# Turning the first stage's fourteen masks by DMA instead of on TensorE, in a four-layer graph network on one core

## Chip, core and metric

One core of one Trainium2 chip runs the whole program. The metric is the device time of one execution in microseconds (us); before the change the median of three runs is 2909.86 us (2909.22 to 2911.19).

## The reference, cut to what matters

The inputs are `x` (2708 x 512, float32) and an adjacency matrix `adj` (2708 x 2708, int32, symmetric, about 2.3% ones). Four layers follow each other, each `x = layernorm(x + gnn(x, adj))`. Only the first layer bears on the change:

```
Ab = adj > 0
keep = Ab & (cumsum(Ab, axis=1) <= 64)          # the first 64 neighbours of each row
nb_mean = (keep @ x) / max(keep.sum(axis=1), 1)
xj = leaky_relu(nb_mean @ W_nb.T + b_nb)
xi = leaky_relu(x @ W_line.T + b_line)
x = layernorm(x + xi + where(cnt > 0, xj, 0))
```

The second layer uses `Ab` without the limit of 64; the third and fourth are attention layers over the same mask.

## The kernel before

The 2708 rows are cut into 22 tiles of up to 128 rows (`NT = 22`, `P = 128`; the last tile, `LAST = 21`, has 20 rows). The kernel keeps the transposed mask of the whole graph in one fp8 tile, `maskT`, with the columns of one tile of rows side by side. The first layer has two stages.

**First stage** (the loop `for t in range(NT)` under `l0a`). For each tile `t` of rows:

- TensorE transposes the rows of `x` (four 128x128 blocks, line L133) and ScalarE copies them out as `xT` (L135). This is done one tile ahead.
- TensorE multiplies `xT` by `W_nb.T` (L259, "the first product" below). ScalarE writes the result rounded to fp32r as `yH` (L231) and VectorE the rest as `yL` (L236).
- TensorE multiplies `xT` by `W_line.T` (L259, "the second product"). VectorE adds the bias (L363) and applies leaky ReLU (L195); POOL's queue stores the result (L365). The second product has one PSUM buffer, so that of tile t+1 waits for the bias addition of tile t.

Beside this, 14 of the 22 masks (`HERE = NT - 8`) are made in this stage, at t = 2 to 6, 8 to 12 and 14 to 17 ("mask iterations"); t = 7, 13 and 18 to 21 make none, and t = 7 and t = 13 are called gaps here. For one mask of 128 rows:

- POOL's queue loads it from `adj` as bf16 (L272) into a buffer `m`, one of three.
- ScalarE takes a sigmoid over all 2708 columns, which also counts the ones (`count`, L277).
- VectorE runs a scan and a multiplication over the first half of the columns, and again over the second half (`place`, L283 and L286). The first scan waits for `count`; the scan of the second half continues the first. They are called scan 1, multiplication 1, scan 2 and multiplication 2.
- `turn_here` transposes the finished mask on TensorE in 22 blocks (L295) into PSUM, and ScalarE takes the sign of what stands there, in four pieces (8, 8, 5 and 1 blocks, L299), into `maskT`. POOL's queue then copies a few rows of the last block (L302).

**Second stage** (`l0b`). The masks' columns of four tiles at a time are expanded by ScalarE (`kept`, L380) and TensorE accumulates mask x (yH + yL) over all 22 tiles (L516). The remaining 8 masks are made beside it by `other_masks`, and these are turned by DMA already: `turn` (L307, on SP's queue) writes the transposed blocks into free memory, and `signs` (L312) is ScalarE's pass from there into `maskT`.

The order on each engine is fixed when the program is built: a scheduler lays the instructions out in each engine's queue, and each queue is worked off in order at run time. A few orders are forced by hand: `pe` ties TensorE's instructions of the first stage into the order in which they are written, and `tc.issue_after` holds `count` and `place` behind named instructions.

Of the kernel before, what the change touches and what calls it, by code (L numbers as in the profile page):

```python
# [2 lines left out]

# [27 lines left out]
def kernel(  # L31
# [18 lines left out]
    def rows(t):  # L50
        return min(P, N - t * P)
# [151 lines left out]
    with ExitStack() as phase:  # L203
# [5 lines left out]
        gate = yp.tile([P, 1], F32, name="gate")  # L209
        nc.vector.memset(gate, -STEP / 2)  # L210
        weight2 = yp.tile([P, KD, D], F32, name="weight2")
        yH = yp.tile([P, NT, D], F32R, name="yH")
        yL = yp.tile([P, NT, D], F32R, name="yL")
        nc.gpsimd.memset(yH[:, NT - 1, :].bitcast(F32), 0.0)
        nc.gpsimd.memset(yL[:, NT - 1, :].bitcast(F32), 0.0)

        ps_tr = phase.enter_context(tc.tile_pool(name="ps_tr", bufs=2, space=PSUM))
        ps_mm = phase.enter_context(tc.tile_pool(name="ps_mm", bufs=1, space=PSUM))
# [9 lines left out]
        highs = {}  # L228

        def keep_y(t, n, pm):  # L230
            highs[t] = nc.scalar.copy(yH[:n, t, :], pm[:n])  # L231
            if t == LAST:
                low = slice(TWIN, TWIN + n)
                nc.scalar.copy(yL[low, t, :], pm[low])
                return nc.vector.tensor_sub(yH[low, t, :], pm[low], yL[low, t, :].bitcast(F32))
            return nc.vector.tensor_sub(yL[:n, t, :], pm[:n], yH[:n, t, :].bitcast(F32))  # L236

        def halves(j):

# [30 lines left out]
        def load_mask(i, m):  # L270
            n = rows(turns[i])
            nc.gpsimd.dma_start(m[:n, :N], adj[turns[i] * P:turns[i] * P + n, :], max_dma_last_dim=N * 2)  # L272
            return m
# [11 lines left out]
                                         OP.add, OP.min)  # L285
            return nc.vector.tensor_mul(m[:n, c0:c1], m[:n, c0:c1], places[:n, :c1 - c0])  # L286

        def turn_here(i, m, psum, order=as_it_comes):
            t, n = turns[i], rows(turns[i])
            for g0 in range(0, NT, G):  # L290
                g1 = min(g0 + G, NT)
                ps = psum()
                for j in range(g0, g1):
                    w = rows(j)
                    order(nc.tensor.transpose(ps[:w, j - g0, :n], m[:n, j * P:j * P + w], identb[:n, :n]))  # L295
                parts = [(P, g0, min(g1, FULL))] + ([(rows(FULL), FULL, NT)] if g1 > FULL else [])
                for w, a, b in parts:
                    if a < b:
                        nc.scalar.activation(maskT[:w, a:b, t * P:t * P + n], ps[:w, a - g0:b - g0, :n], AF.Sign,  # L299
                                             saturate=False)  # L300
                if g1 == NT:
                    nc.gpsimd.dma_start(maskT[TWIN:TWIN + few, LAST, t * P:t * P + n],  # L302
                                        maskT[:few, LAST, t * P:t * P + n])
                yield

        def turn(i, m, into):
            nc.sync.dma_start_transpose(into, m)  # L307

# [11 lines left out]
        with ExitStack() as ph:  # L320
            st = ph.enter_context(tc.tile_pool(name="l0a", bufs=1))
            wnT, wlT = weight(), weight2
            room = [maskT[:, G + k, :4 * D].bitcast(F32) for k in range(2 * KD)]

            xs = rows_of(x)
            xTs = early(0, NT, lambda t, order=as_it_comes: transposed(ahead, ps_tr, xs(t), rows(t), "xT", order))

            transpose_weight(room[:KD], ps_tr, wnT, l0_w_nb, (nc.sync, nc.scalar))  # L330
            lows = {}
            for t in range(2):
                xT = xTs(t, order=pe)
# [3 lines left out]
            masks = early(1, HERE, lambda i: load_mask(i, st.tile([P, N], BF16, name="m", bufs=3)))  # L337
# [3 lines left out]
            counted = turned = 0  # L341
            for t in range(NT):
                n = rows(t)
                if t > 1:

                    lows[t] = keep_y(t, n, product(xTs(t, order=pe), n, wnT, 0, pe, sums() if t % 2 else None))
                xT = xTs(t)
                if t + 1 < NT:
                    xTs(t + 1, order=pe)
                while turned < counted - (t + 2 < NT):  # L350
                    for _ in turn_here(turned, masks(turned), lambda: sums(BF16, (P, G, P)), pe):
                        pass
                    turned += 1
# [9 lines left out]
                nc.vector.tensor_add(u[:n], pm[:n], b_line[:n])  # L363
                low = rows_made = leaky(u[:n], u[:n])
                nc.gpsimd.dma_start(r0_dram[t * P:t * P + n, :], u[:n])  # L365
                if now:
                    with tc.issue_after(low.ins):
                        place(counted, m, places, 1, 2)
                    counted += 1

        with ExitStack() as ph:
# [132 lines left out]
            for i, b in enumerate(cuts):  # L506
                ts_ = range(*b)
                pa = {t: sums() for t in ts_}
                for j in range(NT):
                    if j + 1 < NT:  # L510
                        nxt, nxt_made = kept(b, j + 1)
                    elif i + 1 < len(cuts):
                        nxt, nxt_made = kept(cuts[i + 1], 0)
                    for t in ts_:
                        for y in halves(j):
                            nc.tensor.matmul(pa[t], kT[:, (t - b[0]) * P:(t - b[0] + 1) * P], y[:, j, :],  # L516
                                             start=(j == 0 and y is yH), stop=(j == LAST))
# [12 lines left out]
                todo = finish(ts_, us)  # L530
# [23 lines left out]
        with ExitStack() as ph:  # L554
            st = ph.enter_context(tc.tile_pool(name="l1b", bufs=2))
            for t in range(NT):
                n = rows(t)
                x1 = fetched(x1_dram, t, n, st, "x1")
                z1 = fetched(z1_dram, t, n, st, "z1")
                pa = sums()  # L560
                for g0 in range(0, NT, G):
                    g1 = min(g0 + G, NT)
                    mf = st.tile([P, G, P], F32R, name="mf")
                    nc.scalar.copy(mf[:, :g1 - g0, :], maskT[:, g0:g1, t * P:(t + 1) * P])  # L564
                    for j in range(g0, g1):
                        for y in halves(j):
                            nc.tensor.matmul(pa, mf[:, j - g0, :], y[:, j, :],  # L567
                                             start=(j == 0 and y is yH), stop=(j == LAST))
# [959 lines left out]
```

## Time and profile before

| What | Value |
|---|---|
| Median of three runs | 2909.86 us (2909.22 to 2911.19) |
| The profiled execution's own time | 2911.22 us |
| Its span on the core | 2909.0 us |
| TensorE busy | 2827.0 us, 97% of the span |
| VectorE busy | 1983.5 us, 68% |
| ScalarE busy | 1501.7 us, 52% |
| POOL busy | 247.5 us, 9% |
| Mean granted TensorE clock | 0.996 |

The first stage takes the first 207 us of the span. The rest is not touched by the change. Shares over the whole span are averages over stages with different limits, so the first stage has to be read by itself: in stretches of time, and instruction by instruction on each engine's timeline.

### The profile page before, as it was taken

To read this page: it belongs to the slowest core of one execution; us is meant where nothing else is said; L and a number is where in the kernel's file an instruction comes from. 1 tells how busy PE (TensorE), PEld (TensorE's weight loads), DVE (VectorE), ACT (ScalarE), POOL (GpSimd) and SP (SyncE) were. 2 spreads that over 40 slices of the span, in tenths; PEclk is the share of its full clock that TensorE was granted. 3 is DMA by queue.
4 is the path that set the end of the run, shared out by engine and by line. 5 is a ranking of instruction groups with operands and counts; after the bars stand their busy time and mean duration, and the time that the engine had idled before them with its cause. 6 is when DMAs were issued, how large, how long until landed. Compare 5 with 4: busy or idle time off the path is not lost. (4 is left out here: it accounts for less than half of the span.)

```text
span 2909.0 us, 36145 instructions
## 1 busy us (share of the span) xinstructions
PE 2827.0 (97%) x14194; PEld 1576.5 (54%) x14194; DVE 1983.5 (68%) x2341; ACT 1501.7 (52%) x1749; POOL 247.5 (9%) x395
## 2 busy tenths in 40 slices
PE   8999999999999999999999999999999999999997
PEld 4457766458887434444466433444375555555555
DVE  6966737442334999999978999999954435435342
ACT  3546632122323999999955999999950000000001
POOL 1111110101110000000022000000200010100001
PEclk9999999999999999999999999999999999999999
DMA  5635536322222011111153111110171000000000
GB/s 134 129 86 121 139 110 176 112 65 93 77 75 78 27 37 37 35 46 47 34 155 107 37 37 40 47 45 34 35 179 42 4 29 11 26 15 16 15 22 21
DMA packets 145301, 187.33 MB, mean 64 GB/s; under 512 B 65791, under 2 KB 90692, under 8 KB 145122
## 3 DMA queue, kind: packets, MB, share of 16 engines
q1 hardware_dynamic: 115254, 123.27, 14.5%
q0 software_dynamic: 18864, 57.45, 7.0%
q10 hardware_dynamic: 11004, 4.22, 0.6%
q8 instruction: 114, 1.87, 0.3%
q14 instruction: 65, 0.53, 0.1%
HBM read 148.91 MB, written 44.65 MB: 67 GB/s over the span
## 5 line engine op out<-in xcount | busy, mean ns | idle before, releaser
L772 DVE SCALAR_TENSOR_TENSOR e<-v_bc,ucol,maskT 128x1408 f32<-128x1408 f32 (+3 forms) x804 | 1133.4, 1472 | 320.2 <-PE pn L1155 312.1
L801 ACT ACTIVATE c<-e,bcol 128x1300 fp8e4<-128x1300 f32 (+2 forms) x688 | 956.6, 1412 | 61.9 <-DVE e L772 16.7
L973 PE MATMUL po<-e,R 128*64 128x512 f32 (+3 forms) x4224 | 893.7, 548 | 25.9 <-DVE e L772 23.8
L973 PEld LDWEIGHTS po<-e,R 128*64 128x64 f32 (+1 forms) x4224 | 333.8, 136 | 552.7 <-issue 389.9
L1155 PE MATMUL pn<-e,R 128*128 128x512 f32 (+3 forms) x1056 | 403.0, 545 | 1.1 <-DVE lin L1175 0.4
L1155 PEld LDWEIGHTS pn<-e,R 128*128 128x128 f32 (+1 forms) x1056 | 183.9, 190 | 197.1 <-issue 181.5
L1105 ACT ACTIVATE w<-pl,b 128x256 f32<-128x256 f32 (+1 forms) x88 | 41.0, 466 | 370.9 <-PE pl L1103 370.9
L516 PE MATMUL acc<-yH,kT 128*128 128x512 f32 x484 | 194.5, 407 | 8.1 <-ACT kT L380 6.0
L567 PE MATMUL acc<-yH,mf 128*128 128x512 f32 x484 | 185.0, 389 | 0.0
L516 PE MATMUL acc<-yL,kT 128*128 128x512 f32 x462 | 181.1, 392 | 0.0
L567 PE MATMUL acc<-yL,mf 128*128 128x512 f32 x462 | 179.7, 389 | 0.0
L122 POOL TENSOR_TENSOR ln_rs<-ln_rs,half 128x1 f32<-128x1 f32 (+1 forms) x88 | 55.4, 630 | 1340.9 <-DVE ln_rs L121 1334.1
L694 PE MATMUL pm<-w,xT 128*128 128x264 f32 (+1 forms) x704 | 165.2, 388 | 2.8 <-DVE R L712 1.2
L259 PE MATMUL pm<-weight,xT 128*128 128x512 f32 (+1 forms) x344 | 156.7, 598 | 9.4 <-DVE u L363 8.0
L1103 PE MATMUL pl<-lin 128*128 128x256 f32 (+1 forms) x704 | 155.9, 376 | 3.4 <-DVE lin L1002 3.4
L1128 PE MATMUL pl<-lin,w 128*128 128x512 f32 x336 | 150.8, 593 | 0.0
L1103 PEld LDWEIGHTS pl<-lin 128*128 128x128 f32 x704 | 131.2, 193 | 34.6 <-issue 15.8
L694 PEld LDWEIGHTS pm<-w,xT 128*128 128x128 f32 (+1 forms) x704 | 129.7, 190 | 25.7 <-ACT xT L135 3.5
L564 ACT CAST mf<-maskT 128x1024 fp32r<-128x1024 fp8e4 (+1 forms) x66 | 64.5, 977 | 151.5 <-PE acc L567 148.2
L259 PE MATMUL pm<-w,xT 128*128 128x512 f32 x296 | 133.4, 593 | 3.3 <-ACT xT L135 2.1
L380 ACT ACTIVATE kT<-maskT 128x512 fp32r<-128x512 fp8e4 (+1 forms) x132 | 77.7, 593 | 103.8 <-PE acc L516 102.1
L873 PE MATMUL pd<-c,parts_c 128*12 128x384 fp8e4 (+2 forms) x2688 | 128.3, 307 | 0.0
(250 smaller groups left out, 2629.1 us busy)
## 6 DMA issues: line engine op xcount, KB each, us to landing
rows<-x_dram SPq DMA_DIRECT2D x63, 256.0 KB
v_bc<-v_dram SPq DMA_DIRECT2D x16, 704.0 KB
rows<-in_x_dram SPq DMA_DIRECT2D x42, 256.0 KB
x_dram<-u POOLq DMA_DIRECT2D x42, 256.0 KB, 2.4
v_bc<-v_dram SPq DMA_DIRECT2D x16, 650.0 KB
m<-in_adj_dram POOLq DMA_DIRECT2D x13, 677.0 KB, 7.1
r_dram<-u POOLq DMA_DIRECT2D x21, 256.0 KB, 2.3
rows<-r_dram SPq DMA_DIRECT2D x21, 256.0 KB
```

What stands on the lines that cost most here:

```text
L259: order(nc.tensor.matmul(pm[:m], xT[:, k, :m], w[:, k, :], start=(k == 0), stop=(k == KD - 1)))
L380: made = nc.scalar.activation(kT[:, :w], maskT[:, j, b[0] * P:b[0] * P + w], AF.Relu, scale=-1.0)
L516: nc.tensor.matmul(pa[t], kT[:, (t - b[0]) * P:(t - b[0] + 1) * P], y[:, j, :], start=(j == 0 and y is yH), stop=(j == LAST))
L567: nc.tensor.matmul(pa, mf[:, j - g0, :], y[:, j, :], start=(j == 0 and y is yH), stop=(j == LAST))
L694: nc.tensor.matmul(pm[a][:m, :D // 2 + heads], xT[:, k, :m], w[:, k, a, :D // 2 + heads], start=(k == 0), stop=(k == KD - 1))
L772: self.made = nc.vector.scalar_tensor_tensor(e[:, :w], v[:, :w], ucol[:, j, h:h + 1], maskT[:, j, c0:c0 + w], op0=OP.max, op1=OP.mult)
L801: nc.scalar.activation(c[:, :w], e[:, :w], AF.Sigmoid, bias=bcol[:, j, h:h + 1], scale=STEP, saturate=False)
L873: pe(nc.tensor.matmul(p[32 * g:32 * g + 12, :c1 - c0], parts_c[:, j, h, :], c[:, c0:c1], start=(i == 0 and h == hs[0]), stop=(i == NT - 1 ...
L973: pe(nc.tensor.matmul(po[i][HO * k:HO * k + HO, :c1 - c0], R2[at, j, h * HO:(h + 1) * HO], e[at, a:a + c1 - c0], start=(i_ == 0), stop=(i_ ...
L1103: nc.tensor.matmul(pl[:, :w], self.lin1[:, k, f * P:(f + 1) * P], h[:, k, :w], start=(k == 0), stop=(k == KD - 1))
L1128: nc.tensor.matmul(pl[:n], gT[:, f, (t - t0) * P:(t - t0) * P + n], self.lin2[:, f, :], start=(f == 0), stop=(f == KF - 1))
L1155: nc.tensor.matmul(pn[k][:, :w], R2[at, j, k * P:(k + 1) * P], e[at, :w], start=(j == 0), stop=(j == NT - 1))
```

## The change

The 14 masks of the first stage are turned by DMA, as the other 8 are: `turn_here` with its transposes on TensorE is gone, `turn` and `signs` take its place. The transposed blocks need memory. `yH` and `yL` keep only the first 19 tiles; their last three tiles lie in two tiles named `end`, and until tile 19 is reached these two hold the turned masks 0 to 11 in turn. Masks 12 and 13 are turned into buffers of `m` that have come free. A mask's buffer is now 2816 columns wide, and POOL clears the last 108 (and the whole buffer of the 20-row mask) ahead of the load.

The order in the program text is: mask c is turned at the start of the next iteration (before, `turn_here` came one iteration later), and its signs are written at the end of the iteration after its multiplication 2, one mask behind the turn. The new lines, cut to the core:

```diff
+        END = NT - 3
+        starts, ends = [yp.tile([P, END, D], F32R, name=name) for name in ("yH", "yL")], []
+        def end_tile(dtype):
+            return yp.tile([P, 3 * D * 4 // mybir.dt.size(dtype)], dtype, name="end", tag="end", bufs=2)
+        def part_of(i, t):
+            return starts[i][:, t, :] if t < END else ends[i][:, (t - END) * D:(t - END + 1) * D]
+        yH, yL = (partial(part_of, i) for i in range(2))
...
-        def turn_here(i, m, psum, order=as_it_comes):
...
-                    order(nc.tensor.transpose(ps[:w, j - g0, :n], m[:n, j * P:j * P + w], identb[:n, :n]))
...
+            def mask_rows(i):
+                m = mask_tile()
+                nc.gpsimd.memset(m[:, N:], 0.0)
+                if rows(turns[i]) < P:
+                    nc.gpsimd.memset(m, 0.0)
+                return load_mask(i, m)
+            def turned_tile(i):
+                if i >= HERE - 2:
+                    return mask_tile().rearrange("p (t n) -> p t n", n=P)
+                return end_tile(BF16)[:, :NT * P].rearrange("p (t n) -> p t n", n=P)
+            def turn_next(i):
+                intos[i] = turned_tile(i)
+                turn(i, masks(i), intos[i])
+            def signs_of(i):
+                for _ in signs(i, intos.pop(i)):
+                    pass
...
+                if t == END:
+                    while signed < HERE - 2:
+                        signs_of(signed)
+                        signed += 1
+                    ends[:] = [end_tile(F32R) for _ in range(2)]
+                    for y in (yH, yL):
+                        nc.gpsimd.memset(y(LAST).bitcast(F32), 0.0)
...
-                while turned < counted - (t + 2 < NT):
-                    for _ in turn_here(turned, masks(turned), lambda: sums(BF16, (P, G, P)), pe):
-                        pass
+                while turned < counted:
+                    turn_next(turned)
                     turned += 1
...
+                while signed < (HERE if t == NT - 1 else turned - 1):
+                    signs_of(signed)
+                    signed += 1
```

In the built program of the changed kernel the scheduler has put ScalarE's instructions of the first gap and of the tail in this order (`sign c/k` is piece k of the signs of mask c; `yH t` and `xT t` are the copies of tile t):

```
... yH 7, xT 8, sign 3/2, 3/3, 3/4, sign 4/1 [waits for the DMA of mask 4],
    yH 8, xT 9, count 5, sign 4/2, 4/3, 4/4, yH 9, xT 10, count 6,
    sign 5/1 [waits for the DMA of mask 5], yH 10, xT 11, count 7, ...
... sign 12/2, 12/3, 12/4, sign 13/1 [waits for the DMA of mask 13],
    yH 19, xT 20, sign 13/2, 13/3, 13/4, kept, kept, yH 20, xT 21, ...
```

On VectorE it has put the bias addition of most mask iterations in front of scan 1; before, it stood behind it.

More of the change, by code (lines that the diff above doesn't have):

```diff
@@ L1 @@
 from contextlib import ExitStack, nullcontext
+from functools import partial
 from itertools import chain
@@ L211 @@
         weight2 = yp.tile([P, KD, D], F32, name="weight2")
[L212 to L215, printed above, removed]
+        END = NT - 3
[5 more added lines that the diff above has]
+        yH, yL = (partial(part_of, i) for i in range(2))
         ps_tr = phase.enter_context(tc.tile_pool(name="ps_tr", bufs=2, space=PSUM))
@@ L230, in keep_y @@
         def keep_y(t, n, pm):
-            highs[t] = nc.scalar.copy(yH[:n, t, :], pm[:n])
+            highs[t] = nc.scalar.copy(yH(t)[:n], pm[:n])
             if t == LAST:
                 low = slice(TWIN, TWIN + n)
-                nc.scalar.copy(yL[low, t, :], pm[low])
-                return nc.vector.tensor_sub(yH[low, t, :], pm[low], yL[low, t, :].bitcast(F32))
-            return nc.vector.tensor_sub(yL[:n, t, :], pm[:n], yH[:n, t, :].bitcast(F32))
+                nc.scalar.copy(yL(t)[low], pm[low])
+                return nc.vector.tensor_sub(yH(t)[low], pm[low], yL(t)[low].bitcast(F32))
+            return nc.vector.tensor_sub(yL(t)[:n], pm[:n], yH(t)[:n].bitcast(F32))
         def halves(j):
@@ L286, in place @@
             return nc.vector.tensor_mul(m[:n, c0:c1], m[:n, c0:c1], places[:n, :c1 - c0])
-        def turn_here(i, m, psum, order=as_it_comes):
[L289 to L304, printed above, removed]
         def turn(i, m, into):
@@ L336, with mask_tile @@
             b_line = bias(bcast(l0_b_line, D))
-            masks = early(1, HERE, lambda i: load_mask(i, st.tile([P, N], BF16, name="m", bufs=3)))
+            def mask_tile():
+                return st.tile([P, NT * P], BF16, name="m", bufs=3)
+            def mask_rows(i):
[8 more added lines that the diff above has]
+                return end_tile(BF16)[:, :NT * P].rearrange("p (t n) -> p t n", n=P)
+            masks = early(1, HERE, mask_rows)
+            intos = {}
+            def turn_next(i):
[4 more added lines that the diff above has]
+                    pass
             masks(0)
@@ L340 @@
             nc.gpsimd.memset(maskT[:, :, N:], 0.0)
-            counted = turned = 0
+            counted = turned = signed = 0
             for t in range(NT):
                 n = rows(t)
+                if t == END:
[5 more added lines that the diff above has]
+                        nc.gpsimd.memset(y(LAST).bitcast(F32), 0.0)
                 if t > 1:
@@ L515 @@
                         for y in halves(j):
-                            nc.tensor.matmul(pa[t], kT[:, (t - b[0]) * P:(t - b[0] + 1) * P], y[:, j, :],
+                            nc.tensor.matmul(pa[t], kT[:, (t - b[0]) * P:(t - b[0] + 1) * P], y(j),
                                              start=(j == 0 and y is yH), stop=(j == LAST))
@@ L566 @@
                         for y in halves(j):
-                            nc.tensor.matmul(pa, mf[:, j - g0, :], y[:, j, :],
+                            nc.tensor.matmul(pa, mf[:, j - g0, :], y(j),
                                              start=(j == 0 and y is yH), stop=(j == LAST))
```

## The prediction

> **What bounds the first stage now.** TensorE is 97% busy over the span, but that says nothing of these 207 us, so I read the busy time by stretches first (columns: length, then busy us of PE, PEld, DVE, ACT and POOL, the granted clock, the DMA share, GB/s).
>
> ```profile
> 100.00:140.00 40.00, 38.13 (x176) 20.25 (x175) 39.62 (x37) 24.84 (x34) 7.78 (x13) 1.00 0.63 127
> 180.00:220.00 40.00, 38.43 (x136) 20.27 (x135) 17.98 (x21) 13.94 (x28) 6.23 (x15) 1.00 0.37 91
> ```
>
> From 100 to 140 us VectorE is busy 39.62 of 40 us: it sets the pace where masks are made. After the last mask (from 184 us) it is half idle and TensorE sets the pace. The timelines of VectorE, TensorE and ScalarE through the second gap (t = 13) show how the engines hold each other:
>
> ```profile
> 121.33 2.97 DVE L283 TENSOR_TENSOR_SCAN places<-m,over 128x1354 bf16<-128x1354 bf16 x1
> 130.89 2.97 DVE L283 TENSOR_TENSOR_SCAN places<-m,over 128x1354 bf16<-128x1354 bf16 x1
> 139.06 0.86 DVE L286 TENSOR_TENSOR m<-m,places 128x1354 bf16<-128x1354 bf16 x1
> 143.20 0.69 DVE L236 TENSOR_TENSOR yL<-pm,yH 128x512 fp32r<-128x512 f32 x1 [1.35 <-ACT yH L231]
> 146.23 2.98 DVE L283 TENSOR_TENSOR_SCAN places<-m,over 128x1354 bf16<-128x1354 bf16 x1 [2.34 <-ACT m L277]
> ```
>
> ```profile
> 133.26 1.49 PE L295 MATMUL acc<-identb,m 128*128 128x128 bf16 x22
> 135.41 3.70 PE L259 MATMUL pm<-weight,xT 128*128 128x512 f32 x8 [0.66 <-DVE u L363]
> ...
> 193.95 1.50 PE L295 MATMUL acc<-identb,m 128*128 128x128 bf16 x22
> 195.38 3.70 PE L259 MATMUL pm<-weight,xT 128*128 128x512 f32 x8
> ```
>
> ```profile
> 142.58 0.59 ACT L231 CAST yH<-pm 128x512 fp32r<-128x512 f32 x1 [5.92 <-PE pm L259]
> 143.07 0.59 ACT L135 COPY xT<-ps_tr 128x512 f32<-128x512 f32 x1
> 143.55 2.56 ACT L277 ACTIVATE m<-m,gate 128x2708 bf16<-128x2708 bf16 x1
> ```
>
> To be seen: scan 1 to scan 1 takes 9.56 us (121.33 to 130.89) with VectorE never idle, while TensorE, having done the 22 transposes, still waits 0.66 us for VectorE. In a gap VectorE runs out of work and idles 1.35 + 2.34 = 3.69 us: it waits for the first product, then `yH`, then `count`. The first gap, at 88 to 93 us, shows the same two waits.
>
> What a turn by DMA costs is seen in the second stage. SP issues it, and ScalarE or POOL is released when it lands:
>
> ```profile
> 223.71 3.48 SPq L307 DMA_TRANSPOSE weight<-spare  x1
> 229.02 1.06 ACT L312 ACTIVATE maskT<-weight 128x1024 fp8e4<-128x1024 bf16 x1 [2.09 <-DMA weight<-spare]
> ...
> 317.51 3.33 SPq L307 DMA_TRANSPOSE weight<-w  x1
> 324.61 0.19 POOL L389 MEMSET w<- 128x108 bf16 x1 [7.93 <-DMA weight<-w]
> ```
>
> So 5.3 us from issue to release; 7.1 us in the worst case, where two loads of rows followed in SP's queue. The other turns that release a waiting instruction give 5.2 to 5.3.
>
> **1. The transposes removed.** 22 transposes hold TensorE 1.43 us (193.95 to 195.38); 14 masks make 20.0 us. Thirteen of them lie where VectorE sets the pace, and there TensorE would wait longer instead. Only mask 13's, at 193.95, stands in the tail: -1.4 us on the path.
>
> **2. The new wait on ScalarE.** The sign pass itself is no dearer: 1.06 us for 8 blocks from SBUF, against 2.64 us for the four pieces from PSUM (about 1.0 for the first). But its first piece now waits for the DMA, and it stands ahead of `yH` of the next tile. Behind it are queued `yH`, `xT` and `count`, so VectorE's next scan 1 and TensorE's next first product wait for them. From the end of multiplication 2 of mask c to scan 1 two iterations on, the chain is: release and landing 0.1 + 5.3, sign 1.0, `yH` 0.49 and `xT` 0.48 (142.58 to 143.55), `count` 2.68 (143.55 to 146.23): 10.05 us. From scan 1 to the end of multiplication 2 are 9.0 us (130.89 to 139.92).
>
> Inside a run of masks this loop holds two masks: 10.05 + 9.0 = 19.05 us against VectorE's own 2 x 9.56 = 19.12. It just fits. The new order on VectorE (addition ahead of scan 1) helps a little: an iteration whose addition parted scan 1 from multiplication 1 took 9.34, not 9.56. Beyond 5.3 us the loop binds. I charge 0.7 us once, in the first run, where `sign 0/2` to `1/3` crowd ScalarE too, and no gain.
>
> In a gap the chain is paid in full. Before, from the last scan 1 of the run to the next one: 146.23 - 130.89 = 15.34 us. After: 9.0 + 10.05 = 19.05, or +3.7. The bias addition that followed that scan (0.62) is then already done and the next iteration shorter, but the chain that starts at its end takes most of that back: I take +3.5. Two gaps: +7.0.
>
> **3. The tail.** Before, from the end of multiplication 2 of mask 13 (182.89 + 0.86 = 183.75) to the end of the stage (206.89): 23.14 us. After, `xT` 20 stands behind `sign 13/1`, and the first product of tile 20 waits for `xT`: 0.1 + 5.3 + 1.0 + 0.49 + 0.65 = 7.54 us. In the trace that product starts at 190.07, 16.82 us before the end; less the transposes, 15.4. Together 22.9: -0.2. What TensorE saves, ScalarE's wait takes.
>
> Sum with turns that land in 5.3 us: 0.7 + 7.0 - 0.2 = +7.5 us.
>
> **4. Contention.** A mask's load now waits for the turn of the mask three earlier and is issued right behind its landing, about 5.8 us after multiplication 2. The load of 117.82 us shows the DMA engines full from 120 to 123.5 and released `count` at 124.50. So the new load fills the engines until some 11 to 12 us after multiplication 2, while the next turn begins to move data at 9.4 + 0.1 + 1.3. About 1 us of overlap in the eight turns inside runs; shared evenly it lengthens a turn by 0.5 to 1 us. Each us there costs five pairs of iterations about 0.9 each: +2.5 to +4.5. I take +3.5. The bounds are nothing, and 7.1 us for every turn: (7.1 - 5.3) x (5 x 0.9 + 2 gaps + tail) = 1.8 x 7.5 = +13.5.
>
> **5. Edits at nothing.** POOL's clears (0.19 us each) stand ahead of loads that have over 4 us to spare. SP is held 3.4 us by a turn, and waits for multiplication 2 first; queued behind are loads of `x` rows, needed more than an iteration later. The load of mask 14 waits for the last turn and signs, near 201 us instead of 195.65; its `count` comes at about 217, and a load takes 7. Uncovered, each of these would cost its excess, at most 2 us once.
>
> **6. The clock.** Two idle stretches of 1.6 us on TensorE at 225 and 229 us were followed by a granted clock of 0.5 from 232 to 235.4 us; one of 2.11 us at 60.9 was not. After each gap TensorE will stand idle some 4 us before one second product, since the addition it waits for now comes behind the next `count` and scan 1. A drop there doubles a 3.45 us product; VectorE has most of that covered, so 0 to +2 us each, +4 in all at most. I take 0. The Trainium skill ("TensorE: Matmul & The Clock Gate", HAM oscillation) puts the limit at idle gaps of about 3.4 us; the stretch at 225 us, with shorter ones, says the limit can lie lower. By the page a stall of 4 us would mostly drop the clock, and the sum would be nearer +13 than +11.
>
> A rule that speaks against the change is in the skill's "VectorE: DVE Perf Modes" (The three transpose paths): 1309 ns for a 128x128 block by DMA against 390 ns on TensorE, and TensorE preferred where PSUM will do. The trace has 22 blocks in 5.3 us by DMA and in 1.43 on TensorE, so the direction holds. By the page's figure 22 blocks would take 28.8 us, an estimate that the landing times exclude here.
>
> **Sum.** +7.5 + 3.5 = +11.0 us. The profiled execution took 2911.22 us (span 2909.0); it would become 2922.2. It lies 1.4 us above the median of the runs, so I put 2909.86 + 11.0 = 2920.9.
>
> **Rivals.** *A: VectorE's pace and TensorE's relief win (faster).* If a turn lands before ScalarE comes to its signs, nothing holds `yH`. Then each gap loses about 1.8 of its idle time, since TensorE has the next first product ready early (-3.6), the second product of tile 19 follows VectorE at once, 0.7 us instead of 2.97 after multiplication 2 (-2.3), the transposes go (-1.4) and the order on VectorE gives 1: about -8, 2902. It decides below some 3.5 us from issue to landing, where two gaps and the tail, at 1 us per us each, have given back the 5 to 6 us. Against it: SP alone is busy 3.3 us with one turn, and none of the seven turns whose landing can be read took under 5.1. Chance 0.05.
> *B: no measurable change.* Landings at 5.2 and the reordered VectorE, worth 0.2 us in nine iterations, take 2 to 4 us off: +3.5 to +5.8, 2913.4 to 2915.6. It needs a turn undisturbed by loads. Chance 0.13.
> *C: contention at its bound*, every turn 7.1 us and the clock dropping in both gaps: 7.5 + 13.5 + 4 = +25, 2935. For it: the one turn of 7.1; against it: at 235.71 and 276.05 us loads followed too, and those landed in 5.3. Chance 0.12. The forecast, +6 to +16, keeps 0.70.
>
> A measurement of this kernel can tell about 0.2%, 5.8 us, from no change: slower means over 2915.7. That is the forecast and C, 0.82; same 0.13; faster 0.05. The range leaves out A, the lower part of B and the end of C: 2913 to 2933.
>
> **What would show it.** Right: on ScalarE's timeline the first sign piece of a mask waits for the DMA in nearly every mask iteration, `yH` follows directly, and VectorE's idle time in the gaps rises from 3.7 to about 7.5 us; TensorE's idle time in the first stage grows by about 30 us (20 of transposes, 11 of length); the second stage starts 8 to 14 us later and runs as before. Wrong: sign pieces that find their data landed; scan 1 to scan 1 at 9.3 us in runs with gaps below 3.7 (A); spacings of 10.5 us and turns of 7 us (C); or the second stage stalling anew at its first mask.

## The result and the profile after

The changed kernel takes 2937.16 us (median of four runs, 2934.69 to 2940.09) against 2910.53 us for the kernel before on the same chip. The ratio is 1.0091, with a 95% interval of 1.0073 to 1.0108: 26.6 us slower. The forecast was +11.0 us (2920.9), with a range up to 2933. So the sign was right and the size was not: the loss lies 4 us beyond the range.

The profiled execution after took 2934.69 us, with a span of 2932.8 us, 23.8 us more than before. First the same look by stretches (columns: length, then busy us of PE, PEld, DVE, ACT and POOL, the granted clock, the DMA share, GB/s), after the change:

```profile
100.00:140.00 40.00, 28.23 (x67) 12.19 (x66) 29.45 (x26) 21.76 (x27) 5.41 (x11) 0.93 0.75 150
```

VectorE, which had been busy 39.62 of these 40 us, is busy 29.45, and TensorE 28.23 instead of 38.13. Neither sets the pace any longer, and TensorE's clock now falls at times (0.93). What went up is the share of the DMA engines (0.63 to 0.75) and what they moved (127 to 150 GB/s).

Next the second gap of the kernel after, all engines in order of time. Mask 8 is turned from 148.94 us, mask 9 from 158.23:

```profile
148.94 4.03 SPq L296 DMA_TRANSPOSE end<-m  x1
149.31 2.97 DVE L290 TENSOR_TENSOR_SCAN places<-m,over 128x1354 bf16<-128x1354 bf16 x1
154.90 1.06 ACT L301 ACTIVATE maskT<-end 128x1024 fp8e4<-128x1024 bf16 x1 [4.17 <-DMA end<-m]
154.99 0.19 POOL L331 MEMSET m<- 128x108 bf16 x1 [1.26 <-DMA end<-m]
155.47 0.71 POOL L279 DMA_DIRECT2D m<-in_adj_dram  x1 [0.30 <-issue]
157.22 0.85 DVE L293 TENSOR_TENSOR m<-m,places 128x1354 bf16<-128x1354 bf16 x1
158.23 6.08 SPq L296 DMA_TRANSPOSE end<-m  x1
168.88 1.06 ACT L301 ACTIVATE maskT<-end 128x1024 fp8e4<-128x1024 bf16 x1 [10.19 <-DMA end<-m]
169.84 0.57 ACT L238 CAST yH<-pm 128x512 fp32r<-128x512 f32 x1
170.31 0.59 ACT L136 COPY xT<-ps_tr 128x512 f32<-128x512 f32 x1
170.44 0.69 DVE L243 TENSOR_TENSOR yL<-pm,yH 128x512 fp32r<-128x512 f32 x1 [10.97 <-ACT yH L238]
170.78 2.56 ACT L284 ACTIVATE m<-m,gate 128x2708 bf16<-128x2708 bf16 x1
173.47 2.98 DVE L290 TENSOR_TENSOR_SCAN places<-m,over 128x1354 bf16<-128x1354 bf16 x1 [1.74 <-ACT m L284]
```

This is the chain of the forecast, link by link: multiplication 2 ends at 158.07, the turn is issued at 158.23, ScalarE's first sign piece waits for it, and `yH`, `xT`, `count` and scan 1 follow directly. But the turn lands 10.65 us after its issue (168.88 - 158.23), not 5.3. A load of another mask was issued at 155.47, 2.8 us ahead of it, because it had waited for the turn before. VectorE is idle 10.97 + 1.74 = 12.71 us in this gap; before it was 3.69.

Where the first stage's 29.5 us went (it ended at 206.89 and now ends at 236.42 us), read from the starts of scan 1 on VectorE's timelines:

| Stretch | Before | After | Difference |
|---|---|---|---|
| Start to the first bias addition | 26.66 | 32.13 | +5.5 |
| First run, scan 1 of mask 0 to mask 4 | 37.71 | 40.90 | +3.2 |
| First gap, mask 4 to mask 5 | 15.35 | 22.95 | +7.6 |
| Second run, mask 5 to mask 9 | 38.18 | 40.34 | +2.2 |
| Second gap, mask 9 to mask 10 | 15.34 | 24.16 | +8.8 |
| Third run, mask 10 to mask 13 | 28.48 | 30.64 | +2.2 |
| Tail, scan 1 of mask 13 to the end | 32.18 | 32.31 | +0.1 |

The rows add up to 29.6; the stretch between the first two rows takes 12.99 us in both. The second stage runs as before; of the offset, 1.1 us come back by 267 us of the kernel after (before, the clock was at half from 232 to 235.4 us; now it isn't there), and the rest of the way to 23.8 us comes back in small steps up to the end of the span, inside the 5.4 us by which the runs of one kernel differ.

The start was no part of the forecast. The kernel after, POOL and VectorE:

```profile
2.68 6.97 DVE L65 CAST identb<-ident 128x128 bf16<-128x128 f32 x1 [1.43 <-POOL ident masks.py:199]
2.70 2.46 POOL L352 MEMSET maskT<- 128x2816 fp8e4 x1
5.08 2.46 POOL L333 MEMSET m<- 128x2816 bf16 x1
5.72 3.93 DVE L147 COPY w<-ps_tr 128x512 f32<-128x512 f32 x2
7.47 2.10 POOL L353 MEMSET maskT<- 128x2376 fp8e4 x1
```

and TensorE in the same microseconds, after:

```profile
9.75 1.97 PE L146 MATMUL ps_tr<-ident,maskT 128*128 128x128 f32 x8 [3.21 <-DVE w L147]
11.65 1.11 PE L134 MATMUL ps_tr<-ident,rows 128*128 128x128 f32 x4
13.44 5.94 PE L266 MATMUL pm<-w,xT 128*128 128x512 f32 x8 [0.67 <-ACT xT L136]
```

A cast of 128x128 elements on VectorE seems to take 6.97 us: it ends at 9.65, 0.08 us after the third of POOL's clears. TensorE waits 3.21 us for the copies queued behind it, and then its first product takes 5.94 us instead of 3.70: 3.2 + 2.2 = 5.4 us. The trace of before had a small version of it that I passed over:

```profile
1.70 0.52 POOL L215 MEMSET yL<- 128x512 f32 x1
1.77 0.53 DVE L64 CAST identb<-ident 128x128 bf16<-128x128 f32 x1 [0.52 <-POOL ident masks.py:199]
```

There too the cast ended 0.08 us after the clear (2.30 and 2.22).

### The profile page after: what moved, and what is told of

Its sections match the earlier page's. It is cut to its first block, busy times and chain, and to the rows that moved or that the text cites. A ratio compares the mean times of both kernels' runs of the same rounds, so it can differ in the third digit from the quotient of the medians.

```text
span 2932.8 us, 35607 instructions
## 1 busy us (share of the span) xinstructions
PE 2817.9 (96%) x13886; PEld 1558.4 (53%) x13886; DVE 1988.7 (68%) x2341; ACT 1502.9 (51%) x1749; POOL 252.3 (9%) x410
## 3 DMA queue, kind: packets, MB, share of 16 engines
q1 hardware_dynamic: 155126, 133.36, 16.4%
## 5 line engine op out<-in xcount | busy, mean ns | idle before, releaser
L823 ACT ACTIVATE c<-e,bcol 128x1300 fp8e4<-128x1300 f32 (+2 forms) x688 | 956.7, 1412 | 61.3 <-DVE e L794 16.4
L538 PE MATMUL acc<-yH,kT 128*128 128x512 f32 x418 | 169.7, 406 | 6.7 <-ACT kT L402 4.8
L266 PE MATMUL pm<-w,xT 128*128 128x512 f32 x296 | 142.9, 628 | 23.3 <-ACT xT L136 22.3
L538 PE MATMUL acc<-yL,kT 128*128 128x512 f32 x418 | 163.3, 391 | 0.0
L589 PE MATMUL acc<-yH,mf 128*128 128x512 f32 x418 | 162.7, 389 | 0.0
L589 PE MATMUL acc<-yL,mf 128*128 128x512 f32 x418 | 162.6, 389 | 0.0
```

The lines of the kernel that those rows point to most:

```text
L266: order(nc.tensor.matmul(pm[:m], xT[:, k, :m], w[:, k, :], start=(k == 0), stop=(k == KD - 1)))
L589: nc.tensor.matmul(pa, mf[:, j - g0, :], y(j), start=(j == 0 and y is yH), stop=(j == LAST))
L823: nc.scalar.activation(c[:, :w], e[:, :w], AF.Sigmoid, bias=bcol[:, j, h:h + 1], scale=STEP, saturate=False)
```

## The experiments

Each ratio is to the kernel before, run on the same chip; "worth" is a difference of two ratios times 2911 us. With the intervals of both ratios a worth is good to some 4 to 7 us.

### The start: one edit, a part alone, and the whole start

The cast alone moved (edit to the kernel after):

```diff
-    nc.vector.tensor_copy(identb, ident)
...
+            with tc.issue_after(lows[1].ins):
+                nc.vector.tensor_copy(identb, ident)
```

> The kernel after the change, with one instruction moved: the cast of the identity to bf16 (VectorE, 6.97 us in the profile after) comes behind the second yL instead of first; POOL's clears all stay. Theory 'the cast and the clears share something': only the cast was held, from the start of POOL's string of clears at 2.70 us to its end at 9.57, and everything on VectorE queued behind it. Then the reductions and the copies of the weight run at once, the first bias addition comes at 26.5 to 27.5 us instead of 32.13, and the time falls by about 5 us, to 2931 to 2933. Rival 'the clears hold all of VectorE': the copies are still held until 9.6 us, the first addition stays at 31 to 32, and the time falls by at most 1 us, to 2936 to 2938.

2936.4 us, ratio 1.0084 (1.0070 to 1.0098): hardly any gain. But the profile says that half of the theory holds. The cast now takes 0.22 us, and the copies of the weight run at 5.82 us with 0.69 each beside the same clears, as does the reduction of `ident` (0.64 us, from 2.68), so it was only the cast that the clears held. What takes its place shows on TensorE, kernel with the cast moved:

```profile
9.97 1.09 PE L133 MATMUL ps_tr<-ident,rows 128*128 128x128 f32 x4 [1.43 <-DMA rows<-in_x_dram]
11.73 6.29 PE L265 MATMUL pm<-w,xT 128*128 128x512 f32 x8 [0.68 <-ACT xT L135]
```

TensorE is done with the weight at 8.5 us, as before the change, but the rows of `x` have not landed: the first mask's load is issued at 1.32 us now, ahead of them; before it was issued at 2.17, behind them (POOL cleared parts of `yH` and `yL` first). And the first product is still at half speed.

The mask buffers alone (edit to the kernel before):

```diff
-            masks = early(1, HERE, lambda i: load_mask(i, st.tile([P, N], BF16, name="m", bufs=3)))
+            def mask_rows(i):
+                m = st.tile([P, NT * P], BF16, name="m", bufs=3)
+                nc.gpsimd.memset(m[:, N:], 0.0)
+                if rows(turns[i]) < P:
+                    nc.gpsimd.memset(m, 0.0)
+                return load_mask(i, m)
+            masks = early(1, HERE, mask_rows)
```

> The kernel before, turning on TensorE, with only the mask buffers of the change: 2816 columns wide, the last 108 cleared by POOL ahead of each load, the buffer of the 20-row mask cleared whole. Theory 'the cast and the clears share something': here the identity is made before the first mask's load, so the cast comes at 1.8 us, ahead of the string of clears, and ends by 3 us; the clears of 0.2 us each cost nothing later on. The time stays within 1.5 us of before, 2909 to 2912. Rival 'the clears hold all of VectorE' (or cost something ahead of each load): the first bias addition comes some 5 us later, 2914 to 2917.

2913.03 us, against 2910.83 for the kernel before on this chip: the median lies 1 us above the theory's range, and the ratio is 1.0004 (0.9995 to 1.0013). The first bias addition comes at 26.30 us, no later than before. The same clears cost nothing that can be measured when the cast runs before them (1.77 to 2.42 us). So "edits at nothing" would have been right of the clears as such; it was their place in POOL's queue, ahead of the identity, that cost.

Both waits of the start removed (with the cast moved as above):

```diff
-            masks(0)
             nc.gpsimd.memset(maskT[:, NT - 1, :], 0.0)
-            nc.gpsimd.memset(maskT[:, :, N:], 0.0)
+            cleared = nc.gpsimd.memset(maskT[:, :, N:], 0.0)
+            with tc.issue_after(cleared.ins):
+                masks(0)
```

> The kernel after the change, with the cast of the identity behind the second yL and the clears and loads of the first masks behind POOL's two clears of the big mask tile, so that the first rows of x are in front of the first mask's load again; the rest as after the change. In the run with the cast alone moved, VectorE was no longer held, but TensorE waited 1.43 us for the rows of x instead and its first product took 6.29 us instead of 3.70. Theory 'TensorE starts at half speed and any break in its first microseconds keeps it there': without both waits the first product takes 3.7 us, the first bias addition comes at 26 to 27.5 us (26.66 before, 32.13 after), and the time falls by 5 to 6 us, to 2930 to 2933. Rival 'the first product is slow for another reason': it stays at 5.9 us or more, and the time falls by less than 3 us.

2933.0 us, ratio 1.0071 (1.0058 to 1.0084), worth 5.8 us against the change; with the signs tied (below) the same start is worth 6.4. The time fell as the theory said, but for another reason in part: in the profiled execution the first product, at 10.31 us, still took 5.63 us, although TensorE had had no wait ahead of it, and the first bias addition came at 28.83. Over all profiles of this case (without the last one, which works ahead of it), of eight executions in which TensorE had no wait over 0.7 us ahead of it, six had the first product at 3.70 us and two at 5.4 to 5.6; of five with a wait of 1.4 us or more, all had 5.6 to 6.3. Six of the eight are kernels with this same start: four had 3.70, two 5.4 and 5.6. So the slow start came with every wait, and without one it came in some executions and not in others. A varying start fits what the Trainium skill says ("TensorE: Matmul & The Clock Gate", Part 1: The HAM clock gate): the clock rises after a busy window of about 3.4 us, and the window runs freely, so that the same kernel starts at different points of it.

### The in-order wait and the loads

The sign pieces tied behind `count` (edit to the kernel after; `count` returns its instruction):

```diff
+                last = highs[t]
                 if now:
...
-                        count(counted, m)
+                        last = count(counted, m)
...
-                while signed < (HERE if t == NT - 1 else turned - 1):
-                    signs_of(signed)
+                while signed < (HERE if t >= END else turned - 1):
+                    with tc.issue_after(last.ins):
+                        signs_of(signed)
```

> The kernel after the change, with the sign pieces tied behind the count of the iteration in which the text has them (and in iterations without a mask behind yH), and those of mask 13 written from tile 19 on; turns, loads and clears stay. Theory 'in-order wait on ScalarE': the sign pieces then find their data landed or wait where nothing urgent stands behind them. Scan 1 to scan 1 over the gaps falls from 22.95 and 24.16 us to 15.3 to 16.5, the three runs from 40.90, 40.34 and 30.64 us to 38, 38 and 28.5, the half-speed stretches in the first stage behind the gaps go away, and the start keeps its 5.5 us: 2912 to 2918. Rival 'the transfers themselves set the pace': turns of 7 to 10 us hold the loads, the loads the counts and these VectorE; only the half or less comes back, 2925 to 2933.

2923.11 us, ratio 1.0032 (1.0021 to 1.0044): worth 17.2 us, the largest single part. The runs are back at 9.35 us a mask, as expected, but for the iteration right behind each gap (11.54 and 11.02); the gaps are not (18.2 and 24.3 us). In the later part of the first two runs the turns land 8 to 18 us after their issue, and the gap pays for it. The slowest turn, that of mask 8, from SP's, POOL's and ScalarE's timelines of this kernel, and the DMA share by stretches (next to last column):

```profile
142.45 7.82 SPq L296 DMA_TRANSPOSE end<-m  x1
142.63 0.73 POOL L279 DMA_DIRECT2D m<-in_adj_dram  x1 [0.30 <-issue]
160.35 2.83 ACT L301 ACTIVATE maskT<-end 128x1024 fp8e4<-128x1024 bf16 x4 [14.55 <-DMA end<-m]
163.09 0.56 ACT L238 CAST yH<-pm 128x512 fp32r<-128x512 f32 x1
```

```profile
100.00:165.00 65.00, 49.06 (x118) 22.16 (x119) 49.45 (x45) 34.33 (x44) 11.73 (x25) 0.90 0.96 162
```

A load was issued 0.2 us behind the turn, and the turn landed after 17.9 us. Inside the gap `yH` still stands behind the sign pieces. The verdict lies between the two theories: the in-order wait is a cause, and not the only one.

The loads left out (edit to the kernel after; masks 3 and 5 to 13 are computed from the remains of earlier masks):

```diff
+            ms = [st.tile([P, NT * P], BF16, name=f"m{k}") for k in range(3)]
...
+                m = mask_tile(i)
+                if i == 3 or i > 4:
+                    return m
```

> The kernel after the change, with the loads (and clears) of masks 3 and 5 to 13 left out: these masks work on what the earlier masks left in the three buffers, with the sign of count's scale turned, so that the order on the engines stays and only the loads beside the turns are gone. Theory 'turns are lengthened by loads in flight': all turns release ScalarE 5.2 to 5.5 us after their issue, as in the second stage before; the runs take 38 to 38.5 us, the gaps 19 to 19.5 each, and the time falls by 13 to 18 us, to 2919 to 2924. Rival 'a turn is slow here by itself, or for what stands in SP's queue': landings of 7 us and more stay without loads, and the time falls by less than 4 us.

2925.43 us, ratio 1.0046 (1.0032 to 1.0060), worth 13.1 us, at the edge of what was expected. One load is left beside a turn, that of mask 4, issued at 69.4 us. SP's queue:

```profile
63.76 3.33 SPq L297 DMA_TRANSPOSE end<-m  x1
73.47 4.63 SPq L297 DMA_TRANSPOSE end<-m  x1
82.27 3.37 SPq L297 DMA_TRANSPOSE end<-m  x1
```

The turn beside it holds SP 4.63 us and lands after 6.8; the others hold SP 3.3 to 3.5 and land after 5.2 to 5.5 (6.2 and 6.3 in the two gaps, beside rows and a store). The gaps take 19.74 us each, against 19.05 in the forecast's chain, so with undisturbed turns the forecast of the gaps was nearly right. By the medians this cause is smaller than the in-order wait, but the intervals of the two ratios overlap.

Both at once:

> Both earlier edits in one: the sign pieces tied behind count, and the loads and clears of masks 3 and 5 to 13 left out (these masks work on what the buffers hold). With the signs tied and the loads kept, turns still took 8 to 18 us from issue to landing in the later part of each run, the DMA engines were 96% busy between 100 and 165 us, and the gaps were 18.2 and 24.3 us. Theory 'two causes, the in-order wait and DMA engines that are full': with both gone the gaps take 15.2 to 16 us, the runs 37.4 to 38.2, 37.4 to 38.2 and 28 to 28.6 us, and what is left of the loss is the start: 2914 to 2919. Rival 'ScalarE's sign passes are themselves too much in a gap': the gaps stay at 17.5 us or more with landings of 5.3 us, 2919 to 2924.

2907.94 us, ratio 0.9986 (0.9978 to 0.9995), below both expectations. The gaps are 14.74 and 14.44 us, the runs 37.49, 37.51 and 28.02, the tail 29.87 instead of 32.18. The scans around the first gap:

```profile
82.25 2.98 DVE L291 TENSOR_TENSOR_SCAN places<-m,over 128x1354 bf16<-128x1354 bf16 x1
96.99 2.98 DVE L291 TENSOR_TENSOR_SCAN places<-m,over 128x1354 bf16<-128x1354 bf16 x1 [2.65 <-ACT m L284]
```

So the two causes add within what can be measured: 17.2 + 13.1, against 30.6 measured together (1.0091 - 0.9986). And the time is lower than expected: the first stage ends at 206.80 us, where it ended before (206.89), although it began 5 us late. With neither the wait nor the loads, the relief of TensorE and the new order on VectorE give back those 5 us; rival A had counted on 8.

What a load and a turn ask of the DMA engines is seen from the DMA queues (q0 carries POOL's transfers, q1 SP's). The kernel before, 40 to 184 us (columns: packets, MB, share of 16 engines' time):

```profile
q0 software_dynamic: 4688, 11.85, 41.2%
q1 hardware_dynamic: 2046, 3.71, 8.9%
```

and after, 45 to 213 us:

```profile
q1 hardware_dynamic: 39070, 13.09, 40.2%
q0 software_dynamic: 4656, 11.85, 36.2%
```

The queue that grows is SP's: from 8.9% of 144 us = 12.8 us of all sixteen engines to 40.2% of 168 = 67.5, for the same rows and 13 turns, so 4.2 us a turn. A turn is made of small packets: 38074 under 512 bytes after, 1082 before, some 2850 a turn. The same sum on the other queue, with the kernel with the loads left out as the second equation (17.6 us for 18 stores and 2 loads there, against 59.3 for 16 and 11 before the change), gives 4.7 us a load and 0.45 a store; rows take 0.85. One mask iteration so asks for 4.7 + 0.45 + 0.85 + 4.2 = 10.2 us of the DMA engines, and VectorE finishes one in 9.35. By this sum the transfers fall behind by about 0.9 us a mask inside a run, and the gap has to wait until they have caught up; the share of 0.96 above goes with it. Part of the delay can also come from the load itself, which starts only when a turn has landed and its buffer is free. A fourth buffer for masks was not tried, so how the loss divides between the late load and the full engines stays open.

### What is left when both the start and the signs are mended

> The kernel after the change with the sign pieces tied behind count and the start of the run above; all loads are kept. If the two losses add, the time is that of the tied signs alone (2923) less 5 to 6 us: 2916 to 2919, still 5 to 8 us over before, since the DMA engines stay full. Rival 'the losses overlap' (an earlier start only moves the loads into the turns sooner): 2920 to 2924.

2913.16 us, ratio 1.0010 (1.0001 to 1.0019): worth 6.4 us against the tied signs alone, so the losses add within what can be measured. It is 0.1% over before, with no turn left on TensorE.

The second product in the PSUM buffers that came free (edit to the run above):

```diff
-                pm = product(xT, n, wlT, 1, pe)
+                pm = product(xT, n, wlT, 1, pe, sums())
```

> As the run above, and the second product goes into the PSUM buffers that the transposes no longer use, so that TensorE need not wait for the bias addition of the tile before and can run ahead of VectorE. Theory 'the DMA engines are the bound': a mask needs some 10.5 us of all 16 engines (load 5, turn 4 to 4.5, rows and store 1.4) against VectorE's 9.35, so 14 masks and 8 tiles without one take 155 us or more of the 167 whatever TensorE does, and the time stays at 2908 to 2919. Rival 'the one PSUM buffer is the bound': VectorE no longer runs dry in the gaps (2 x 3.7 us) and TensorE is ahead in the tail (about 8 us): 2895 to 2905, faster than both kernels.

2917.45 us, ratio 1.0022 (1.0012 to 1.0032). The time lies in the theory's range, and taking away the wait for TensorE's one PSUM buffer gained nothing. The profile of this kernel, by stretches:

```profile
100.00:165.00 65.00, 54.37 (x126) 23.94 (x126) 52.20 (x46) 33.32 (x44) 10.49 (x21) 0.84 0.96 175
```

The DMA engines are busy 0.96 of these 65 us, and the gaps are 24.1 and 23.1 us. TensorE's granted clock was 0.84 there, against 0.97 in the run before it, so a part of the loss against that run may be the clock's.

Two more ways to free the gap. First, no signs in iterations without a mask, which keeps ScalarE from waiting for a turn there (edit to the kernel with tied signs and mended start):

```diff
-                while signed < (HERE if t >= END else turned - 1):
+                while signed < (HERE if t >= END else turned - 1 if now else 0):
```

> As the run with tied signs and mended start (2913), but the iterations without a mask write no signs: those of the last mask of a run come behind the first count after the gap, so nothing on ScalarE waits for a turn inside a gap (13.77 and 7.04 us there in the run before). All turns and loads are kept. Theory 'the DMA engines stay full, ScalarE's wait was one way of many in which that shows': the gaps of 23.5 and 16.6 us become 16 to 18 each, since loads and stores still land late, and the time is 2908 to 2912. Rival 'the wait of ScalarE was all of it': gaps of 15 to 15.5 and 2903 to 2907.

2917.73 us, ratio 1.0027 (1.0018 to 1.0037), outside both expectations. In its profile the gaps are 14.44 us each, but the iterations behind them take 14.78 and 12.97. The wait has moved to VectorE, in front of its bias addition, and to POOL:

```profile
88.61 0.19 POOL L332 MEMSET m<- 128x108 bf16 x1 [8.65 <-DMA end<-m]
99.47 0.69 DVE L385 TENSOR_TENSOR u<-pm,bias 128x512 f32<-128x512 f32 x1 [5.17 <-DMA r_dram<-u]
```

The profiled first stage is 7 us shorter than with signs in the gap (210.0 against 217.3 us), yet by the ratios the runs are 4.9 us longer. I can't settle that from one profile of each.

Second, a third buffer for `u` (edit to the run above), so that the addition need not wait for that store:

```diff
-                u = sm.tile([P, D], F32, name="u")
+                u = st.tile([P, D], F32, name="u0") if t % 3 == 2 else sm.tile([P, D], F32, name="u")
```

> As the run in which iterations without a mask write no signs, with a third buffer for the second product's result u, so that the bias addition does not wait for the store of two tiles before. In that run scan 1 to scan 1 was 14.44 us over each gap, but 14.78 and 12.97 us in the iteration behind it: VectorE's bias addition waited 5.17 us there for the store of u, and POOL had issued that store behind the clear of a mask's buffer, which waited 8.65 us for a turn. Theory 'POOL's queue carries the turn's delay to the store': the iterations behind the gaps fall to 9.4 to 11 us, the time by 5 to 8 us. Rival 'the DMA engines are full and another transfer is then the late one': another wait for a DMA takes its place (a count for its load, yL for rows), and the time falls by less than 3 us.

2915.16 us, ratio 1.0015 (1.0004 to 1.0026), about 3 us better, though the intervals overlap. The iterations behind the gaps fell to 10.24 and 9.34 us, as the theory said. No addition waits for a store any more, and another transfer is the late one, a mask's load, for which `count` now waits (ScalarE, this kernel):

```profile
132.30 2.55 ACT L283 ACTIVATE m<-m,gate 128x2708 bf16<-128x2708 bf16 x1 [8.58 <-DMA m<-in_adj_dram]
```

From the scan before it to the scan that this `count` releases are 14.78 us. That is the rival's picture: with the engines nearly full, one wait was taken away and the next transfer in line carried it.

### Six masks on TensorE again

`turn_here` is put back for masks 1, 3, 4, 7, 9 and 11, on top of the run with no signs in the gaps:

```diff
+            on_pe = (1, 3, 4, 7, 9, 11)
...
+                while here < counted - (t + 2 < NT):
+                    if here in on_pe:
+                        for _ in turn_here(here, masks(here), lambda: sums(BF16, (P, G, P)), pe):
+                            pass
+                    here += 1
```

> As the run above, and six of the fourteen masks (1, 3, 4, 7, 9 and 11: the last two of the first run, the last of the second and single ones between) are turned on TensorE again, with their signs from PSUM as before the change. Theory 'the DMA engines are full': their demand per mask falls from about 10.5 us to about 8.3 on the mean, under VectorE's 9.35, so the eight turns land in 5.3 to 7 us, runs keep 9.35 us a mask, gaps fall to 14.5 to 15.5, and the first stage ends at 201 to 206 us (206.89 before): 2903 to 2910, at best just faster than before. Rival 'mixing costs ScalarE and TensorE more than it saves': 2910 to 2915.

2908.93 us, ratio 0.9999 (0.9990 to 1.0008): the time of before. The DMA share over 42 to 192 us is 0.72, against 0.85 in the run it is built on and 0.88 with signs in the gaps, and the gaps are 14.44 and 17.11 us. The time lies in the theory's range, but the first stage ends at 209.0 us in the profile, not at 201 to 206.

With eight matmuls ahead of the first transposes:

```diff
...
+            for _ in range(8):
+                pe(nc.tensor.matmul(ps[:, 0, :], ones, ones, start=True, stop=True))
             transpose_weight(room[:KD], ps_tr, wnT, l0_w_nb, (nc.sync, nc.scalar))
```

> As the run above, with eight matmuls of a tile of ones on TensorE ahead of the first transposes, whose result nobody reads: TensorE then works from about 1.1 us instead of 4.7. In the profile before the first product ran at full speed (3.70 us), in six profiles of changed kernels at half speed for most of it (5.58 to 6.33), with and without breaks ahead of it. Theory 'the clock rises only after a stretch of work whose start is a matter of chance': with the longer stretch the first product takes 3.6 to 3.8 us, and the time is 1 to 3 us under that of the run above. Rival 'no such stretch decides': no difference beyond 1 us.

2906.95 us, ratio 0.9990 (0.9981 to 0.9999), the only version with all loads whose interval lies under the time of before, by 2.9 us, about half of what a measurement of this kernel can tell from no change. The first product took 3.70 us, from 9.52 us on. The medians (2 us apart, with intervals that overlap) go with the theory, but do not show it: the profiled execution itself, 2913.55 us, was the slowest of the eleven although its first product was fast.

## Why the forecast was wrong, point by point

**1 and 3, transposes and tail: right.** The tail, from the end of multiplication 2 of mask 13 as in the forecast, went from 23.14 to 23.54 us (212.88 to 236.42): +0.4, forecast -0.2.

**2, the new wait on ScalarE: the mechanism right, the gap right for a turn of 5.3 us.** Without loads the gaps took 19.74 us; the chain said 19.05. Tying the signs behind `count` gave back 17.2 us, so the wait is shown to be a cause, by the medians the largest. Inside the runs the loop "just fits" only for 5.3 us.

**4, contention: this is the step that failed most.** The forecast took 1 us of overlap and turns of 5.8 to 6.3 us, +3.5 us in all; the fourteen turns took 5.2 to 10.65 us to land, 6.9 on the mean, and leaving out the loads gave back 13.1 us, close to the bound (+13.5). By the table, the runs lost 7.6 us against 4.2 forecast (0.7 + 3.5) and the gaps 16.4 against 7.0. Taking the loads' 13.1 and the start's 5.8 off the 26.6 leaves 7.7 us, if they add, against the +7.5 that points 1 to 3 gave. Two things were missed. The overlap was read off a fixed timetable, with every load 5.8 us behind multiplication 2; but a load waits for a landing, so a late turn makes a late load, which lies deeper in the next turn. And I compared the length of transfers where the load on the engines had to be added up: 10.2 us a mask against 9.35.

**5, "edits at nothing": wrong by 5.5 us in the profile, 5.8 in the medians.** It was asked whether each clear delays its load, not what else uses POOL, or what the load now stands in front of. The Trainium skill has the rule ("SBUF — State Buffer", SBUF: two separate sides): VectorE and POOL share a pair of SBUF ports, and of a POOL instruction and a VectorE instruction in a two-port mode the one that starts first locks the other out for its whole length. The trace doesn't show in which mode an instruction ran; it shows the cast held, and neither the reduction nor the copies. And it goes further than the page: the cast was held over three clears in a row, 6.97 us, not for the one that had begun.

**6, the clock: half right.** Taken as 0, with the drop named as possible, for a second product. It came at first products, which wait for `xT` behind the sign piece: six in the first stage took 5.3 to 5.4 us, each after a wait of 2.9 to 5.1. A wait of one length does not always do the same: 2.11 us was followed by 3.70 at 62.99 us before, and by 5.36 at 62.62 us with wide masks alone. In the second gap the product at 170.95 us took 5.40 us, after a wait of 4.70, but VectorE waited for `count` there, not for TensorE. At the start, where TensorE is alone on the path, half speed cost 2.2 us.

**Rivals.** C (2935) had the time nearly right, and its turns of 7.1 us on the mean (6.9 measured), but in part by luck: it holds nothing for the start, and 4 us for a clock that VectorE did not wait for in the second gap; I gave it 0.12, since two turns of the second stage with loads behind them had landed in 5.3. Those were loads of rows, 256 KB each, and not masks. A's gains exist, some 5 us in the first stage, and showed only in the run without the wait and the loads.

**Signs named in advance.** First sign pieces that wait in nearly every iteration, and `yH` directly behind: yes. VectorE's idle time in the gaps 7.5 us: 11.6 and 12.7. TensorE's idle time in the first stage +30 us: 206.9 - 190.9 = 16.0 before, 236.4 - 186.3 = 50.1 after, +34. Second stage 8 to 14 us later: 29.5.

## What to carry to other kernels

When work moves from an engine to DMA, add up the time of all DMA engines per iteration, the new transfers included, and hold it against the pace of the slowest engine: where the sum was larger, as here, waits appeared wherever a transfer was last in line, and taking one away mostly moved it. Put an instruction that waits for a DMA behind everything urgent in its engine's queue, since the queue is worked off in order. And look at what a small clear or load now stands in front of, at the start above all, where nothing hides it.

## What the runs showed of the hardware

A cast from fp32 to bf16 in SBUF on VectorE was held as long as POOL's clears followed each other (6.97 us; 0.22 alone), while copies out of PSUM (0.69) and a reduction (0.64) ran beside the same clears at their usual length. A turn of a 128x2816 mask by DMA took 4.2 us of all sixteen DMA engines in some 2850 small packets, nearly as much as the load of the mask from `adj` (4.7), and both got slower together: with the signs tied, 17.9 us from issue to landing for a turn issued 0.2 us from a load (mask 8), and 10.5 us for the median load issued from 138 to 166 us (6.8 before the change). TensorE's first product took 3.70 us or 5.4 to 5.6 in starts without a wait that were otherwise equal.
